# Mamba block on one core: the gate moved behind the transpose of y, with features on partitions

## The chip, the core and the metric

The kernel runs on one core of a Trainium2 chip. The core has a matrix engine (PE, with its weight loads shown apart as PEld), a vector engine (DVE), a scalar engine (ACT), a general engine (POOL) and a queue that issues most transfers (SP). Each engine works through its own instructions in the order in which the program gives them, and waits on semaphores for what the others produce. [...]POOL doesn't read PSUM in this kernel. The metric is the device time of one execution in microseconds (us); lower is better.

## The reference, cut to what matters

The input is x, 8 sequences of 512 tokens with 128 features. After a layer norm, x goes through two branches that are added to it: a bidirectional Mamba block and a mixture of 8 experts. Only the end of the Mamba direction is touched by the change:

```
xz = x @ in_w.T ; xi, z = split(xz)            # 256 features each
xi = silu(causal_conv(xi))
delta, B, C = functions of xi
h[t] = h[t-1] * exp(delta[t] * A) + delta[t] * xi[t] * B[t]    # 16 states per feature
y = sum over states of h * C  +  xi * D
y = y * silu(z)                                 # the gate
out_dir = y @ out_w.T
...
out = concat(out_f, out_b) @ combine_w.T + combine_b + residual
```

The backward direction does the same on the reversed sequence, and its output is reversed again. The experts pick one of eight for each token and compute `down(silu(gate x) * up x)`.

## The kernel before, in words

**Units and steps.** There are 16 units, one for each pair of sequence and direction (unit 0 is the forward direction of sequence 0, unit 1 its backward direction, and so on: even units are forward). A unit has 16 steps, one for each state. In step s the kernel computes for both halves (128 features on partitions, 512 tokens along the free axis) the decays exp(delta*A) on ACT (`decay`, L771), two scans over time on DVE (`scan`, L818), the multiplication by C on POOL (`times_c`, L841, tile hs), and the sum over states on PE: every 128x128 block of hs is transposed and accumulated in PSUM into py (`sum_up`, L855), so that py has tokens on partitions. The scan's other input, the tile b, comes from PE. In odd steps ACT scales blocks (`scaled`, L787, tile dbt) and PE transposes them (L800); in even steps PE spreads a row (L805) and DVE multiplies (`product`, L812). (The first and the last unit split this differently.) ACT, PE's part for b, and the loads of C run up to three steps ahead of the scan.

**The order of the work.** No scheduler moves anything: the loop from L1113 on writes out the order. Beside the state loop a plan holds small jobs for each step and place: "ev" and "ev2" at a step's start, "late" after `scaled(s+3)`, "pe0", "dv" after the step's scans and products, "pe" and "pe2" at its end. Jobs at the same place run in the order in which they were planned: first those of `prepare` (the next unit's inputs), then those of `conclude` (the end of the unit before), then those of the experts.

**Preparing the next unit.** While unit u runs its states, `prepare` builds unit u+1: input transposed (L563, L565, tile xin) and projected (`inner`, L575), the convolution in step 2 at "dv" (`conv`, L590: six DVE instructions), also in step 2 at "pe" the projection of z (`gates`, L599, tile pz), and in step 3 at "ev2" the silus on ACT (`silu`: L608 for u, L610 for z, with table loads around them). Later come px (L619), pd (L650), the logarithm's parts on POOL (L689, L691), delta (L698) and du (L709), and PE's transposes of du (L714).

**Concluding the unit before.** After unit u is summed, in the steps of unit u+1:

- step 2 "dv": `gate`, L881: two DVE multiplications of py (PSUM, tokens on partitions) by z into yt (SBUF). That is the last reader of py, which has a single buffer of two banks.
- steps 3 and 4 "pe2": `back`, four blocks each transposed by PE into pyb: L887 for the forward direction (transposes), L889 for the backward one (a matmul with the exchange matrix, which also reverses the tokens within a block).
- steps 4 and 5 "ev": `back_end`, L906: ACT copies pyb to y.
- steps 7 and 8 "pe": `project`, L914 into po; in forward units each half ends with a one-row float32 matmul that adds the bias (L921).
- step 9 "dv": `total`, L929, adds po to xt.

The last unit has no unit after it and runs the same in two pairs of blocks (`by_pairs`, L931).

**Shared buffers.** All small PE products (pz, pg of the experts, pyb, px, pbt, pd, po, pdu ...) take turns in a pool `ps_mm` of two PSUM banks, in program order. In steps 2 to 5 the order is pz, pz, pg, pyb, px, pyb, pbt. So each of them waits for the reader of the tile two places before it.

**The experts.** From unit 4 on, a group of four tiles of sorted tokens is worked on for each unit. What matters here: in step 3 ("ev", before the z silu) ACT does a table load and a silu over the group (`expert_silu`, L477), PE makes pg (L457) at "pe0" of step 3, and DVE multiplies it in at "dv" of step 4 (`expert_up_end`, L481).

Of the kernel before, what the change touches and what calls it, by code (L numbers as in the profile page):

```python
# [32 lines left out]
F32 = mybir.dt.float32  # L33
BF16 = mybir.dt.bfloat16
I32 = mybir.dt.int32
AF = mybir.ActivationFunctionType
# [19 lines left out]
def columns():  # L56

    at, n = {}, 0
    fields = [("ln_g", 1), ("ln_b", 1), ("rout", E)]
    for d in DIRS:  # L60
        fields += [
            ((d, k), w) for k, w in (
                ("in", 2 * DI), ("conv_w", NH * KC), ("conv_b", NH), ("A_log", NH * NS),
                ("D", NH), ("x", NH * NX),
            )
        ]
    for d in DIRS:
# [9 lines left out]
def block_kernel(ctx: ExitStack, tc: tile.TileContext, a: dict, out: bass.AP):  # L77
    nc = tc.nc
# [17 lines left out]
    def mm(shape, name):  # L96
        return ps_mm.tile(shape, F32, tag="mm", name=name)
# [6 lines left out]
    at, width = columns()  # L104
    pk = const.tile([P, width], F32, name="pk")
# [13 lines left out]
    comb_b = pk[0:1, at["comb_b"]]  # L119
    w = {}  # L120
    for i, d in enumerate(DIRS):
        w[d, "in"] = pk[:, at[d, "in"]]
# [29 lines left out]
    ones = const.tile([P, P], F32, name="ones")  # L152
# [35 lines left out]
    def selector():  # L188


        nothing = const.tile([P, 1], F32, name="nothing")
        nc.vector.memset(nothing, 0.0)
        for k in range(3):
            nc.gpsimd.affine_select(
                out=sel,
                in_=sel if k else nothing[:ROWS].unsqueeze(2).to_broadcast([ROWS, NS, P]), compare_op=ALU.not_equal, fill=1.0,
                base=-k * NS, pattern=[[-1, NS], [0, P]], channel_multiplier=1,
            )

    def project_weights(d, di):  # L200
        mo = const.tile([P, NH, D], F32, name=f"{d}_mo")
        p = mm([P, NH, D], f"pm_{d}")
        for h in range(NH):
            nc.tensor.matmul(
                p[:, h, :], w[d, "out"][:, h * P : (h + 1) * P], comb[:, di, :],
                start=True, stop=True,
            )
        w[d, "mo"] = mo
        return lambda: nc.scalar.copy(mo, p)
# [318 lines left out]
    def prepare(v):  # L528
        b, d = units[v]
# [6 lines left out]
        bank = mm if v else term  # L536
        c = C[v]
# [54 lines left out]
                        cw[:, h, KC - 1 - k : KC - k], c["acc"][:, h, k:], ALU.mult, ALU.add,  # L592
                    )

        def gates(k):
            p = c["pz", k] = bank([P, 2, DI], f"pz_{v}{k}")
            for j in range(2):
                t = (k * 2 + j) * P
                nc.tensor.matmul(  # L599
                    p[:, j, :], c["xin"][:, t : t + P], w[d, "in"][:, DI:],  # L600
                    start=True, stop=True,
                )

        def silu():
            c["z"] = two.tile([P, NJ, DI], F32, tag="z", name=f"z_{v}")
            c["u"] = two.tile([P, NH, L], F32, tag="u", name=f"u_{v}")
            for h in range(NH):
                nc.scalar.activation(c["u"][:, h, :], c["acc"][:, h, :], AF.Silu)  # L608
            for k in range(2):
                nc.scalar.activation(c["z"][:, 2 * k : 2 * k + 2, :], c["pz", k], AF.Silu)  # L610

        def after_silu():

# [109 lines left out]
        do = lambda f, *k: lambda: f(*k)  # L723
# [149 lines left out]
    def conclude(v):  # L873
        b, d = units[v]
        c = C[v]

        def gate(ks=range(0, NJ, 2)):
            if "yt" not in c:
                c["yt"] = tmp.tile([P, NJ, DI], F32, tag="yt", name=f"yt_{v}")
            for k in ks:  # L880
                nc.vector.tensor_mul(  # L881
                    c["yt"][:, k : k + 2], c["py"][:, k : k + 2], c["z"][:, k : k + 2]
                )

        def turned(dst, j, h):
            if d == "f":
                nc.tensor.transpose(dst, c["yt"][:, j, h * P : (h + 1) * P], ident)  # L887
            else:
                nc.tensor.matmul(  # L889
                    dst, c["yt"][:, NJ - 1 - j, h * P : (h + 1) * P], exch,  # L890
                    start=True, stop=True,
                )

        def block(y, h, j):
            return y[:, h, j, :] if len(y.shape) == 4 else y[:, h, j * P : (j + 1) * P]

        def back(h):

            p = c["pyb", h] = mm([P, L], f"pyb_{v}{h}")
            for j in range(NJ):  # L900
                turned(p[:, j * P : (j + 1) * P], j, h)

        def back_end(h):
            if h == 0:
                c["y"] = tmp.tile([P, NH, L], F32, tag="y", name=f"y_{v}")
            nc.scalar.copy(c["y"][:, h, :], c["pyb", h])  # L906

        def project(js=range(NJ), whole=True):
            if whole or js[0] == 0:
                c["po"] = mm([P, NJ, D], f"po_{v}_{js[0]}")  # L910
            p = c["po"]
            for j in js:
                for h in range(NH):
                    nc.tensor.matmul(  # L914
                        p[:, j, :], block(c["y"], h, j), w[d, "mo"][:, h, :],
                        start=(h == 0 and (d == "b" or j == js[0])),
                        stop=(d == "b" and h == NH - 1), skip_group_check=(d == "f"),
                    )
            if d == "f":

                nc.tensor.matmul(  # L921
                    p[:, js[0] : js[-1] + 1, :], ones[0:1, :],
                    comb_b.unsqueeze(1).to_broadcast([1, len(js), D]),
                    start=False, stop=True, skip_group_check=True,
                )

        def total(js=range(NJ)):
            xs = xt[:, b * NJ + js[0] : b * NJ + js[-1] + 1, :]
            nc.vector.tensor_add(xs, c["po"][:, js[0] : js[-1] + 1], xs)  # L929

        def by_pairs():  # L931

            y = tmp.tile([P, NJ, NH, P], F32, tag="y", name=f"y_{v}")
            c["y"] = y.rearrange("p j h t -> p h j t")
            pairs = [range(k, k + 2) for k in range(0, NJ, 2)]
            for i, js in enumerate(pairs):
                gate((NJ - 2 - js[0],) if d == "b" else (js[0],))
                p = c["pyb", i] = mm([P, 2, NH, P], f"pyb_{v}{i}")
# [3 lines left out]
                copy = nc.scalar.copy if i == 0 else nc.vector.tensor_copy  # L942
                copy(y[:, js[0] : js[-1] + 1], p)
# [18 lines left out]

# [49 lines left out]
    for g, ks in enumerate(groups):  # L1012
# [35 lines left out]
    for _ in roots_of_both(nc.vector, 0, NJ):  # L1048
        pass
    weights("f")  # L1050
    selector()
    first.norm()
    first.turn()
    first.turn_end()
# [31 lines left out]
    for h in range(NH):  # L1086
        k = slice(h, h + 1)
# [122 lines left out]
```

## Time and profile before

| | |
|---|---|
| time, median of 3 runs | 952.93 us (952.07 to 959.26) |
| the profiled execution, its own time | 953.34 us |
| its span on the core | 951.6 us |
| busy: DVE / PE / POOL / ACT | 907.2 / 850.2 / 841.5 / 803.0 us |
| mean granted clock of PE | 0.953 |

One execution is profiled. Rows of the timeline give the start, the length, the engine, the source line, what is written and read, how many like instructions were merged, and in brackets how long the engine sat idle before and what released it. Instructions on DVE and ACT overlap a little: the next one starts some 0.1 us before the one before is reported as ended. So the time that an instruction takes from its engine is read from the distance of two starts.

### The profile page before, as it was taken

The page shows a single profiled execution, that of the slowest core. Times are in us where ns is not written, and L with a number is a line of the kernel's source. Part 1 is how long each engine was busy: PE and PEld are TensorE (multiplying, and loading weights), DVE is VectorE, ACT ScalarE, POOL GpSimd, SP SyncE. Part 2 cuts the span into 40 slices and gives each one's busy share as a digit, 9 for nine tenths or more (in the row PEclk, how much of TensorE's full clock was granted, in tenths as well). Part 3 has the DMA queues.
Part 4 walks back from the last instruction along what each step waited for, and adds up shares of the span by engine and source line. Part 5 has one row for each costly group of instructions (what it writes and reads, how often), then busy time and mean ns, then how long its engine had stood idle before and what let it go on. Part 6 is the DMA issues. An engine that isn't in the chain of part 4 may idle for free.

```text
span 951.6 us, 16224 instructions
## 1 busy us (share of the span) xinstructions
PE 850.2 (89%) x5510; PEld 657.9 (69%) x5510; DVE 907.2 (95%) x1101; ACT 803.0 (84%) x1490; POOL 841.5 (88%) x524
## 2 busy tenths in 40 slices
PE   5699896978789889899998999989999999989897
PEld 2367574766567668777786877868777786767676
DVE  7999989999899999999999999999999999999996
ACT  5898986969679797998969989698988979799792
POOL 5689798799999979799897998979899898979995
PEclk9588999988979999999899999999999999999999
DMA  5364222222233625245441544425245341622262
GB/s 153 111 132 107 66 76 66 78 74 80 84 95 104 192 70 182 78 123 163 114 154 53 161 138 121 152 82 185 63 130 168 112 153 54 186 74 85 90 177 75
DMA packets 68483, 108.54 MB, mean 114 GB/s; under 512 B 6848, under 2 KB 29248, under 8 KB 68400
## 3 DMA queue, kind: packets, MB, share of 16 engines
q1 hardware_dynamic: 65552, 101.32, 36.0%
q0 software_dynamic: 2272, 4.67, 1.4%
q10 hardware_dynamic: 576, 1.51, 0.5%
q8 instruction: 44, 0.72, 0.3%
q14 instruction: 39, 0.32, 0.1%
HBM read 97.60 MB, written 9.87 MB: 113 GB/s over the span
## 4 chain that ended last, share of the span: by engine, by line
PE 42%; ACT 26%; DVE 18%; issue 7%; POOL 6%; DMA 1%; SPq 0%; POOLq 0%; DVEq 0%; ACTq 0%
PE py L855 14%; DVE hs L818 10%; ACT dA L771 8%; PE b L800 7%; ACT dbt L787 7%; PE pg L457 4%; PE pd L650 4%; POOL hs L841 3%; DVE b L812 3%; DVE acc L590 2%; PE pde L489 2%; PE po L914 2%; PE b L805 2%; ACT acc L582 1%; PE pdu L714 1%
## 5 line engine op out<-in xcount | busy, mean ns | idle before, releaser
L841 POOL TENSOR_TENSOR hs<-hs,cs 128x1024 f32<-128x1024 f32 x253 | 594.3, 2362 | 71.9 <-DVE hs L818 59.9
L818 DVE TENSOR_TENSOR_SCAN hs<-dA,b 128x512 f32<-128x512 f32 x512 | 592.8, 1206 | 0.1
L855 PE MATMUL py<-ident,hs 128*128 128x128 f32 x2048 | 279.3, 282 | 10.8 <-POOL hs L841 10.7
L855 PEld LDWEIGHTS py<-ident,hs 128*128 128x128 f32 x2048 | 234.4, 145 | 47.2 <-POOL hs L841 23.6
L787 ACT ACTIVATE dbt<-dut,bt 128x256 f32<-128x256 f32 x524 | 221.9, 496 | 0.1
L800 PE MATMUL b<-ident,dbt 128*128 128x128 f32 x1048 | 187.5, 289 | 19.6 <-DVE hs L818 10.4
L771 ACT ACTIVATE dA<-delta,b_A 128x512 f32<-128x512 f32 x256 | 168.2, 715 | 14.9 <-DVE hs L818 14.8
L800 PEld LDWEIGHTS b<-ident,dbt 128*128 128x128 f32 x1048 | 128.8, 145 | 74.1 <-ACT dbt L787 52.7
L771 ACT ACTIVATE dA<-delta,f_A 128x512 f32<-128x512 f32 x256 | 168.6, 715 | 8.3 <-DVE hs L818 6.3
L812 DVE TENSOR_TENSOR b<-du,b 128x512 f32<-128x512 f32 x250 | 159.8, 686 | 9.3 <-PE b L805 8.5
L599 PE MATMUL pz<-pk,xin 128*128 128x256 f32 x128 | 42.8, 492 | 29.3 <-DVE acc L590 25.4
L650 PE MATMUL pd<-cdt,pk 9*128 9x512 f32 x124 | 66.3, 635 | 0.0
L590 DVE SCALAR_TENSOR_TENSOR acc<-pi,pk,acc 128x511 f32<-128x511 f32 (+2 forms) x96 | 64.5, 739 | 0.1
L457 PE MATMUL pg<-xeT,we 128*128 128x128 f32 x468 | 61.8, 278 | 2.2 <-ACT z L610 2.1
L457 PEld LDWEIGHTS pg<-xeT,we 128*128 128x128 f32 x468 | 56.2, 192 | 5.5 <-ACT z L610 3.8
L599 PEld LDWEIGHTS pz<-pk,xin 128*128 128x128 f32 x128 | 30.2, 247 | 41.1 <-ACT dbt L787 26.5
L805 PE MATMUL b<-cdt,sel 48*128 48x512 bf16 x125 | 50.6, 405 | 8.6 <-DVE hs L818 8.6
L721 ACT COPY dut<-pdu 128x512 f32<-128x512 f32 x32 | 18.6, 585 | 34.6 <-PE pdu L714 34.6
L500 POOL DMA_INDIRECT by_token<-ye,to x39 | 39.6, 1016 | 6.3 <-issue 3.1
L646 POOL TENSOR_TENSOR cdt<-cdt 32x512 f32<-32x512 f32 (+1 forms) x32 | 33.1, 1034 | 7.8 <-ACT cdt L632 7.7
L489 PEld LDWEIGHTS pde<-we,g 128*128 128x128 f32 x234 | 27.6, 191 | 15.2 <-issue 7.6
L409 POOL DMA_INDIRECT sorted_in<-xn,row_i x32 | 32.5, 1015 | 5.3 <-issue 3.8
(170 smaller groups left out, 1054.8 us busy)
## 6 DMA issues: line engine op xcount, KB each, us to landing
cs<-cd SPq DMA_DIRECT2D x253, 256.0 KB, 3.5
we<-in_expert_w SPq DMA_DIRECT2D x39, 576.0 KB, 4.6
sorted_in<-empty SPq DMA_DIRECT2D x9, 258.0 KB, 7.9
xe<-sorted_in SPq DMA_DIRECT2D x9, 258.0 KB, 4.5
xt<-in_x SPq DMA_DIRECT2D x8, 256.0 KB, 7.3
moe<-by_token SPq DMA_DIRECT2D x8, 256.0 KB, 3.0
out<-xt SPq DMA_DIRECT2D x7, 256.0 KB, 3.7
pk<-in_pack ACTq DMA_DIRECT2D x1, 704.0 KB, 7.9
```

What stands on the lines that cost most here:

```text
L457: nc.tensor.matmul(p[:, q - 4 * b, :], T[ks[i]][:, which, c, :], G[ks[0], "xT"][:, i, :], start=True, stop=True,)
L590: nc.vector.scalar_tensor_tensor(c["acc"][:, h, k:], c["pi", h][:, : L - k], cw[:, h, KC - 1 - k : KC - k], c["acc"][:, h, k:], ALU.mult, ...
L599: nc.tensor.matmul(p[:, j, :], c["xin"][:, t : t + P], w[d, "in"][:, DI:], start=True, stop=True,)
L650: nc.tensor.matmul(p, w[d, "dt"][:, h * P : (h + 1) * P], cdt[ROW_DT : NX + 1], start=True, stop=True,)
L771: nc.scalar.activation(k["dA"][:, h, :], c["delta"][:, h, :], AF.Exp, scale=w[d, "A"][:, h, n : n + 1],)
L787: nc.scalar.activation(k["dbt"][:, j, :], c["dut"][:, j, :], AF.Copy, scale=c["bt"][:, j, n : n + 1],)
L800: nc.tensor.transpose(k["b", h][:, j * P : (j + 1) * P], k["dbt"][:, j, h * P : (h + 1) * P], ident,)
L805: nc.tensor.matmul(k["b", 0], sel[:, n, :], c["bc"], start=True, stop=True)
L812: nc.vector.tensor_mul(k["b", h], c["du"][:, h, :], k["b", 0])
L818: nc.vector.tensor_tensor_scan(k["hs"][:, h, :], k["dA"][:, h, :], k["b", h], 0.0, ALU.mult, ALU.add)
L841: nc.gpsimd.tensor_mul(k["hs"], k["hs"], k["cs"].unsqueeze(1).to_broadcast([P, NH, L]))
L855: nc.tensor.matmul(c["py"][:, j, h * P : (h + 1) * P], block[:, h, j * P : (j + 1) * P], weight, skip_group_check=True, **kw,)
```

## The change

The gate is applied after the transpose instead of before it.

- `gates(h)` computes z with features on partitions: the weights are stationary and xin is moving, two matmuls 512 wide in place of four 256 wide. z then has the layout of u (features by tokens), and three buffers instead of two.
- `leave` (step 2, "late") copies py to yt by one ACT instruction over both banks. DVE no longer has a job for the unit before in step 2.
- `back` uses transposes in both directions; the exchange matrix is no longer used here.
- `gate(h)` (steps 4 and 5, "dv") is a DVE multiplication of pyb (PSUM) by z into y. For the backward direction y is written from its last token to its first. It replaces ACT's copies L906.
- `project` starts in forward units with a single matmul of three rows in bf16 over all four blocks, in place of the two float32 matmuls at the end of the halves. The three rows are the bias split in three bf16 pieces, made once at the start by two small POOL subtractions (`bias_pieces`); the packed input holds the bias in three rows.
- `by_pairs` follows the same order for the last unit: two copies out of py (one on ACT, one on DVE), the transposes, two DVE multiplications.

```diff
+    bias = comb_b.bitcast(BF16).rearrange("p (n two) -> p n two", two=2)[:, :, 1]
+    one_row = const.tile([3, P], BF16, name="one_row")
+    nc.gpsimd.memset(one_row, 1.0)
...
+    def bias_pieces():
+        for m in (2, 1):
+            nc.gpsimd.tensor_sub(comb_b[:m], comb_b[:m], bias[:m])
...
-        def gates(k):
-            p = c["pz", k] = bank([P, 2, DI], f"pz_{v}{k}")
-            for j in range(2):
-                t = (k * 2 + j) * P
-                nc.tensor.matmul(
-                    p[:, j, :], c["xin"][:, t : t + P], w[d, "in"][:, DI:],
-                    start=True, stop=True,
-                )
+        def gates(h):
+            p = c["pz", h] = bank([P, L], f"pz_{v}{h}")
+            nc.tensor.matmul(
+                p, w[d, "in"][:, DI + h * P : DI + (h + 1) * P], c["xin"],
+                start=True, stop=True,
+            )
...
-            c["z"] = two.tile([P, NJ, DI], F32, tag="z", name=f"z_{v}")
+            c["z"] = two.tile([P, NH, L], F32, tag="z", name=f"z_{v}", bufs=3)
...
-        def gate(ks=range(0, NJ, 2)):
+        def leave(copy=nc.scalar.copy, js=range(NJ)):
             if "yt" not in c:
                 c["yt"] = tmp.tile([P, NJ, DI], F32, tag="yt", name=f"yt_{v}")
-            for k in ks:
-                nc.vector.tensor_mul(
-                    c["yt"][:, k : k + 2], c["py"][:, k : k + 2], c["z"][:, k : k + 2]
-                )
+            k = slice(js[0], js[-1] + 1)
+            copy(c["yt"][:, k], c["py"][:, k])
 
         def turned(dst, j, h):
-            if d == "f":
-                nc.tensor.transpose(dst, c["yt"][:, j, h * P : (h + 1) * P], ident)
-            else:
-                nc.tensor.matmul(
-                    dst, c["yt"][:, NJ - 1 - j, h * P : (h + 1) * P], exch,
-                    start=True, stop=True,
-                )
+            nc.tensor.transpose(dst, c["yt"][:, j, h * P : (h + 1) * P], ident)
...
-        def back_end(h):
+        def gate(h):
             if h == 0:
                 c["y"] = tmp.tile([P, NH, L], F32, tag="y", name=f"y_{v}")
-            nc.scalar.copy(c["y"][:, h, :], c["pyb", h])
+
+            y = c["y"][:, h, :] if d == "f" else c["y"][:, h, ::-1]
+            nc.vector.tensor_mul(y, c["pyb", h], c["z"][:, h, :])
...
+            if new and d == "f":
+
+                nc.tensor.matmul(
+                    p, one_row, bias.unsqueeze(1).to_broadcast([3, NJ, D]),
+                    start=True, stop=False, skip_group_check=True,
+                )
...
-            (2, "dv", gate),
-            (3, "pe2", do(back, 0)), (4, "ev", do(back_end, 0)),
-            (4, "pe2", do(back, 1)), (5, "ev", do(back_end, 1)),
+            (2, "late", leave),
+            (3, "pe2", do(back, 0)), (4, "dv", do(gate, 0)),
+            (4, "pe2", do(back, 1)), (5, "dv", do(gate, 1)),
```

More of the change, by code (lines that the diff above doesn't have):

```diff
@@ L118, in block_kernel @@
     comb = halves("comb", D)
-    comb_b = pk[0:1, at["comb_b"]]
+    comb_b = pk[0:3, at["comb_b"]]
+    bias = comb_b.bitcast(BF16).rearrange("p (n two) -> p n two", two=2)[:, :, 1]
+    one_row = const.tile([3, P], BF16, name="one_row")
+    nc.gpsimd.memset(one_row, 1.0)
     w = {}
@@ L608, in silu @@
                 nc.scalar.activation(c["u"][:, h, :], c["acc"][:, h, :], AF.Silu)
-            for k in range(2):
-                nc.scalar.activation(c["z"][:, 2 * k : 2 * k + 2, :], c["pz", k], AF.Silu)
+            for h in range(NH):
+                nc.scalar.activation(c["z"][:, h, :], c["pz", h], AF.Silu)
         def after_silu():
@@ L875, in conclude @@
         c = C[v]
-        def gate(ks=range(0, NJ, 2)):
+        def leave(copy=nc.scalar.copy, js=range(NJ)):
             if "yt" not in c:
                 c["yt"] = tmp.tile([P, NJ, DI], F32, tag="yt", name=f"yt_{v}")
-            for k in ks:
-                nc.vector.tensor_mul(
-                    c["yt"][:, k : k + 2], c["py"][:, k : k + 2], c["z"][:, k : k + 2]
-                )
+            k = slice(js[0], js[-1] + 1)
+            copy(c["yt"][:, k], c["py"][:, k])
         def turned(dst, j, h):
-            if d == "f":
-                nc.tensor.transpose(dst, c["yt"][:, j, h * P : (h + 1) * P], ident)
-            else:
-                nc.tensor.matmul(
-                    dst, c["yt"][:, NJ - 1 - j, h * P : (h + 1) * P], exch,
-                    start=True, stop=True,
-                )
-        def block(y, h, j):
-            return y[:, h, j, :] if len(y.shape) == 4 else y[:, h, j * P : (j + 1) * P]
+            nc.tensor.transpose(dst, c["yt"][:, j, h * P : (h + 1) * P], ident)
         def back(h):
@@ L901, in back @@
                 turned(p[:, j * P : (j + 1) * P], j, h)
-        def back_end(h):
+        def gate(h):
             if h == 0:
                 c["y"] = tmp.tile([P, NH, L], F32, tag="y", name=f"y_{v}")
-            nc.scalar.copy(c["y"][:, h, :], c["pyb", h])
+            y = c["y"][:, h, :] if d == "f" else c["y"][:, h, ::-1]
+            nc.vector.tensor_mul(y, c["pyb", h], c["z"][:, h, :])
         def project(js=range(NJ), whole=True):
-            if whole or js[0] == 0:
+            new = whole or js[0] == 0
+            if new:
                 c["po"] = mm([P, NJ, D], f"po_{v}_{js[0]}")
             p = c["po"]
+            if new and d == "f":
[3 more added lines that the diff above has]
+                )
             for j in js:
@@ L914, in project @@
                     nc.tensor.matmul(
-                        p[:, j, :], block(c["y"], h, j), w[d, "mo"][:, h, :],
-                        start=(h == 0 and (d == "b" or j == js[0])),
-                        stop=(d == "b" and h == NH - 1), skip_group_check=(d == "f"),
-                    )
[L919 to L925, printed above, removed]
+                        p[:, j, :], c["y"][:, h, j * P : (j + 1) * P], w[d, "mo"][:, h, :],
+                        start=(d == "b" and h == 0), stop=(h == NH - 1),
+                        skip_group_check=(d == "f"),
+                    )
         def total(js=range(NJ)):
@@ L931, in by_pairs @@
         def by_pairs():
-            y = tmp.tile([P, NJ, NH, P], F32, tag="y", name=f"y_{v}")
-            c["y"] = y.rearrange("p j h t -> p h j t")
+            c["y"] = tmp.tile([P, NH, L], F32, tag="y", name=f"y_{v}")
+            blocks = lambda t: t.rearrange("p h (j t) -> p j h t", t=P)
             pairs = [range(k, k + 2) for k in range(0, NJ, 2)]
-            for i, js in enumerate(pairs):
-                gate((NJ - 2 - js[0],) if d == "b" else (js[0],))
-                p = c["pyb", i] = mm([P, 2, NH, P], f"pyb_{v}{i}")
+            late = pairs[::-1]
+            for i, js in enumerate(late):
+                leave(nc.vector.tensor_copy if i else nc.scalar.copy, js)
+            for i, js in enumerate(late):
+                k = slice(js[0], js[-1] + 1)
+                p = mm([P, 2, NH, P], f"pyb_{v}{i}")
                 for j in js:
@@ L941, in by_pairs @@
                         turned(p[:, j - js[0], h, :], j, h)
-                copy = nc.scalar.copy if i == 0 else nc.vector.tensor_copy
-                copy(y[:, js[0] : js[-1] + 1], p)
+                nc.vector.tensor_mul(
+                    blocks(c["y"][:, :, ::-1])[:, k], p, blocks(c["z"])[:, k]
+                )
             for js in pairs:
@@ L1051, in block_kernel @@
     selector()
+    bias_pieces()
     first.norm()
@@ L1180 @@
         pack[NX, c] = v["dt_b"]
-    pack[0, at["comb_b"]] = inputs[pre + "combine_b"]
+    pack[:3, at["comb_b"]] = inputs[pre + "combine_b"]
     src["pack"] = pack
```

## The prediction

> **What bounds the kernel now.** I read the page's busy shares first, then DVE's waits, then one unit boundary in the timeline, then POOL's starts against the scans.
>
> ```profile
> PE 850.2 (89%) x5510; PEld 657.9 (69%) x5510; DVE 907.2 (95%) x1101; ACT 803.0 (84%) x1490; POOL 841.5 (88%) x524
> ...
> DVE b L812 <- PE b L805: 8.5, 15, 0.9
> DVE yt L881 <- PE py L855: 2.7, 3, 1.6
> ```
>
> DVE idles 44.4 us of 951.6. By windows of about a unit, 8.6 of that lie in the first 48 us and 8.7 in the last 22; a unit in the middle has 1 to 4. An edit that only moves DVE work can therefore win little, but anything that makes DVE wait costs. The gate hardly waits now (2.7 us in three places).
>
> The boundary at 681 us, in the middle of the run (unit 10, forward, is concluded in unit 11), engine by engine:
>
> ```profile
> 681.18 1.28 DVE L881 TENSOR_TENSOR yt<-py,z 128x512 f32<-128x512 f32 x2
> 682.38 1.21 DVE L818 TENSOR_TENSOR_SCAN hs<-dA,b 128x512 f32<-128x512 f32 x1
> ...
> 688.03 0.67 DVE L481 TENSOR_TENSOR g<-g,pg 128x512 f32<-128x512 f32 x1
> 688.61 1.22 DVE L818 TENSOR_TENSOR_SCAN hs<-dA,b 128x512 f32<-128x512 f32 x1
> ...
> 681.37 1.28 ACT L477 ACT_TABLE_LOAD   x1
> 682.66 1.49 ACT L477 ACTIVATE g<-g 128x1536 f32<-128x1536 f32 x1
> 684.05 1.14 ACT L608 ACTIVATE u<-acc 128x512 f32<-128x512 f32 x2
> 685.09 1.06 ACT L610 ACTIVATE z<-pz 128x512 f32<-128x512 f32 x2
> ...
> 685.72 1.16 PE L457 MATMUL pg<-xeT,we 128*128 128x128 f32 x8
> 686.72 0.60 PE L800 MATMUL b<-ident,dbt 128*128 128x128 f32 x4
> 687.15 0.60 PE L887 MATMUL pyb<-ident,yt 128*128 128x128 f32 x4
> 688.01 1.09 PE L855 MATMUL py<-ident,hs 128*128 128x128 f32 x8
> 688.94 1.45 PE L619 MATMUL px<-u,pk 128*104 128x512 f32 x3
> ```
>
> The reader is to see a chain: ACT goes through table load, expert silu, u and z without a pause; pg starts 0.05 us after the first z (685.67), as it needs that pz bank; b and pyb follow back to back, ready at 687.75. Today only ACT waits for pyb.
>
> **The change, part by part.**
>
> *DVE.* The two multiplications leave step 2 (distance of starts 682.38 - 681.18 = 1.20 us) and two of the same shape come at steps 4 and 5: 0.68 us each as in L881, since an operand in PSUM, one in SBUF and the size stay. Writing backwards is in no row: 0.68 is the nearest row; twice that is my upper end (0.68 x 16 = 11 us), below 0.68 is excluded since the elements are the same. I take 0.68.
>
> *ACT.* Two copies L906 (distance to the next start 0.47 each) go, one of 1024 from PSUM comes. Its row doesn't exist: a 512 copy takes 578 ns, and the SBUF activations L666 went from 630 (512) to 1058 (1024), so 578 + 428 = 1.01 us, less 0.12 overlap = 0.89 on the engine; 0.8 to 1.0 as ends. The total is nil, but the place isn't: it stands in step 2 ahead of the table load. Queued behind it are the expert silu, u and z, and behind z wait PE's pg, b and pyb. It doesn't wait itself: py's last sum ended at 678.1, ACT comes free at 681.37.
>
> *The new wait.* With the copy, z's first half ends at 685.67 + 0.89 = 686.56, pg starts at 686.61, pyb 1.43 later as now (687.15 - 685.72), takes 0.60, and DVE can multiply at 688.69. DVE arrives at 688.03 - 1.20 = 686.83. Stall: 1.85 us; behind it are L481, which also frees the bank for px, and all scans. For a backward unit (boundary at 625) the same: pg 629.53, pyb 630.96, DVE 631.83 - 1.20, as pyb there falls to 0.60 too. At the second multiplication DVE comes 3.4 us of scans and products later, pyb is there.
>
> *What the stall is worth.* Two counts. DVE idles 0.92 us (at 666.96) in the unit from 625 to 681 and 0.37 + 0.24 + 0.46 = 1.07 in the next; these waits are for PE and vanish when DVE is late: 1.85 - 0.92 = 0.93 and 1.85 - 1.07 = 0.78 remain. POOL: from step 5 to the end of du it is busy without a break, and its waits elsewhere show that hs starts 0.24 after the scan at the earliest. In step 7 it starts 1.13 after (698.89 against 697.77), so 0.89 is free and 0.96 of the 1.85 goes on, to du, to PE, which already waits for it in the unit from 625, to xin, to ACT, and to the next boundary:
>
> ```profile
> 664.99 0.66 PE L714 MATMUL pdu<-ident,du 128*128 128x128 f32 x4 [0.50 <-POOL du L709]
> ```
>
> I take 0.95 for a boundary that concludes a backward unit and 0.80 for a forward one, where POOL's du leaves PE 0.15 more.
>
> *PE.* Backward pyb: transposes instead of exchange matmuls. Rows: eight records in 1.06 us against four in 0.60. The Trainium skill (TensorE: Matmul & The Clock Gate, Part 4: PE-mode transpose) puts a transpose in a kernel at about 275 ns and says that it doesn't count as busy for the clock gate: four would be 1.1 us, no gain, with 0.5 more stall in backward units (5 x 0.5 = 2.5 us) and a lower clock. The rows decide: four end to end in 0.60, and the stretch from 629 to 679, mostly transposes, ran at a granted clock of 1.00. Bias: 0.69 twice becomes one three-row bf16 matmul 512 wide, nearest row L805 at 405 ns (0.25 to 0.63 as ends): 0.9 us less in each forward unit. But px now waits for L481: 688.69 + 1.26 = 689.95 against 688.94, 1.0 later. So PE is even at du and the gain is spent. pz: 8 records 1.97, as L575 with 4 records 1.88: nil. If POOL didn't hold PE there, the 0.9 would come out; that is the second rival.
>
> The Trainium skill (Perfetto Trace Analysis, Matmuls) asks to rotate PSUM banks so that evacuation overlaps the next matmuls. pyb is now evacuated by the late DVE and px stands behind; the rule has no price, the row gives the 1.0 above.
>
> *Start.* A memset and two POOL subtractions (nearest POOL rows 0.1 and 0.24 to 0.40) stand behind the selector, where POOL idles 7.7 us until 22.08: nil; uncovered 0.9 us.
>
> **Sum.** Boundaries with an expert silu: units 4 to 13, ten. The first has DVE 0.5 later against ACT, so stall 1.26; there POOL's slack is nil (hs starts 0.23 after the scan) and I take 1.0. Then five backward at 0.95 (4.75) and four forward at 0.80 (3.2): 8.95 in all. The boundaries of units 0 to 3: the first delays POOL by about 1 (logits stand where pg does); the second lets POOL start its saturated stretch 1.2 earlier (171 us) as the gate no longer precedes the scan; the third stalls DVE about 1.1, but DVE idles 4.0 us for POOL at 257. I take 0. Unit 14: 0. Tail: now 943.46 gate, 947.30 first total, 948.23 second. New: copies on ACT and DVE side by side to 944.1, transposes 0.6, multiplication 0.68 to 945.5, four blocks of project 1.06, total at 946.6, the second at 947.65: -0.6.
>
> Span 951.6 + 8.95 - 0.6 = 960.0. The profiled execution took 953.34, 1.7 around the span, so 961.7; the median lies 0.4 below the profiled one: 961 us, 0.9% slower.
>
> **Rivals.**
> - *The stall is paid whole.* DVE is 95% busy and recovers nothing: 10 x 1.85 + 1.3 + 1.1 - 0.6 = +20, 973 us. For: DVE has no idle in many units' first 30 us. Against: the idles that vanish are counted above and are waits for PE. A dearer backward write or copy ends here too.
> - *Faster: PE and POOL set the pace.* POOL starts step 3's product 1.2 earlier, PE saves 0.9 in a forward unit and 0.9 (two times 0.46) in a backward one. If the stall stays below POOL's free 0.89, nothing of it passes on and about 0.9 in 14 units less 0.6 comes out: 940 us. The price falls on POOL's step 7; the point is a stall of 0.9. It would need z to leave ACT 1 us sooner than counted. For: PE is busy without a gap from 685.7 to 735.6. Against: ACT's chain from xin to z has no pause in the row.
> - *Nothing moves.* Slack unseen takes the rest (DVE's 27 us of idle outside start and tail): 953.
>
> **How the numbers follow.** Forecast 0.52, whole stall 0.20, nothing 0.18, faster 0.10. A measurement of this kernel can tell about 1% (9.5 us) from no change; the forecast at 961 lies just inside that, and some 0.2 of its 0.52 beyond. So slower 0.41, same 0.50, faster 0.09. The range: forecast with its ends (0.4 to 1.4 for a boundary: 956 to 967), stretched to the nothing case below and most of the whole stall above: 952 to 972.
>
> **What would show it.** DVE's gate on pyb idle some 1.3 to 1.9 us before it, for PE, at ten boundaries, none at units 1 and 3. ACT's copy of 1024 near 1.0 us without a wait. POOL no longer 3 to 3.7 us idle at step 3 but less, and 1 us at steps 5 or 7. Fewer waits DVE b L812 for PE. px 1 us later against pg. The second total 0.6 earlier against the last scan. Wrong if gate has no wait (then the faster rival), if DVE's idle rises by 20 us (the first), or if writing backwards costs more than 0.7 us.

## The result, and the profile after

The changed kernel takes 968.54 us (median of 4 runs, 966.91 to 968.99) against 952.5 us for the kernel before (median of 4): a ratio of 1.0157, 95% interval 1.0132 to 1.0182. The forecast was 961.0 (952 to 972). The sign and the range hold; the loss is 16 us where 8 were forecast. The profiled execution of the changed kernel took 968.78 us, its span is 967.0 us, 15.4 us more than before.

The page of the changed kernel: the busy line, and the groups of POOL's product and of DVE's new gate (count, busy us, mean ns, then idle just before them and what ended it).

```profile
PE 848.2 (88%) x5358; PEld 643.7 (67%) x5358; DVE 907.3 (94%) x1101; ACT 806.5 (83%) x1475; POOL 843.0 (87%) x527
...
L848 POOL TENSOR_TENSOR hs<-hs,cs 128x1024 f32<-128x1024 f32 x253 | 594.3, 2360 | 88.0 <-DVE hs L825 72.3
...
L904 DVE TENSOR_TENSOR y<-pyb,z 128x512 f32<-128x512 f32 x30 | 20.4, 679 | 25.8 <-PE pyb L891 25.8
```

No engine has noticeably more to do. DVE's busy time is 907.3 against 907.2, so its idle time went from 44.4 to 59.7 us, and the 15.3 between them is the difference of the spans to 0.1. The gate alone waits 25.8 us where it waited 2.7, so 23.1 us of new waiting came in and 7.8 us of other waiting went. What went are waits for PE and POOL, above all those of L698 (L705 now) for POOL: 6.1 us before, 2.5 now. DVE's longest waits now (us in all, times, longest):

```profile
DVE y L904 <- PE pyb L891: 25.8, 14, 3.4
DVE b L819 <- PE b L812: 7.4, 10, 1.7
DVE st L236 <- DMA xt<-in_x: 5.2, 2, 5.0
```

The boundary that stood at 681 us is at 692.6 now (unit 10 concluded in unit 11). The timeline of the changed kernel, ACT, DVE and PE after one another:

```profile
692.62 0.99 ACT L888 COPY yt<-py 128x1024 f32<-128x1024 f32 x1
693.62 1.28 ACT L486 ACT_TABLE_LOAD   x1
694.92 1.49 ACT L486 ACTIVATE g<-g 128x1536 f32<-128x1536 f32 x1
696.31 1.14 ACT L615 ACTIVATE u<-acc 128x512 f32<-128x512 f32 x2
697.35 1.06 ACT L617 ACTIVATE z<-pz 128x512 f32<-128x512 f32 x2
...
694.84 3.44 DVE L825 TENSOR_TENSOR_SCAN hs<-dA,b 128x512 f32<-128x512 f32 x3
700.05 0.69 DVE L904 TENSOR_TENSOR y<-pyb,z 128x512 f32<-128x512 f32 x1 [1.77 <-PE pyb L891]
700.66 0.68 DVE L490 TENSOR_TENSOR g<-g,pg 128x512 f32<-128x512 f32 x1
...
697.98 1.16 PE L466 MATMUL pg<-xeT,we 128*128 128x128 f32 x8 [0.92 <-ACT z L617]
698.97 0.60 PE L807 MATMUL b<-ident,dbt 128*128 128x128 f32 x4
699.41 0.60 PE L891 MATMUL pyb<-ident,yt 128*128 128x128 f32 x4
...
701.20 1.88 PE L626 MATMUL px<-u,pk 128*104 128x512 f32 x4
```

The copy stands ahead of everything, z comes 0.89 us later than before (counted from the end of the convolution: 5.30 against 4.41), PE has run out of other work and waits 0.92 us for z, pg and pyb follow, and DVE, which has given up the two multiplications and is early, stands 1.77 us at the gate. This is the chain of the forecast, with its durations.

Where the 15.4 us lie can be read from the ends of the convolutions in the two timelines, one per unit. Up to the one at 343.10 (before: 341.26) it is +1.84, in the nine periods from there to 866.13 (850.76) +13.53, and from there to the end +0.03. The nine periods follow (f or b: direction of the unit concluded). Beside them stand the stretches in which PE's granted clock was 0.5 instead of 1.0 (3.41 us long, or a multiple), counted where they start 4.7 to 20 us after the convolution, while pyb, px and pd are made. Those at the boundary itself, within 1 us of the convolution's end, are not counted:

| period | before, us | such stretches | after, us | such stretches |
|---|---|---|---|---|
| unit 4, f | 56.13 | | 58.43 | 1 |
| 5, b | 56.20 | | 58.76 | 2 |
| 6, f | 58.29 | 1 | 57.65 | |
| 7, b | 56.47 | 1 | 57.17 | |
| 8, f | 56.72 | | 60.05 | 2 |
| 9, b | 56.19 | | 57.46 | 1 |
| 10, f | 56.72 | | 58.46 | 1 |
| 11, b | 56.17 | | 57.43 | 1 |
| 12, f | 56.61 | | 57.62 | |

Without such a stretch a forward period went from 56.72 to 57.65 (+0.93; unit 12 has +1.01) and a backward one from 56.19 to 57.17 (+0.98). That gives 5 x 0.93 + 4 x 0.98 = 8.6 of the 13.5, about 5 us less than was measured. The changed kernel has a stretch in six of nine periods, the kernel before in two. Held against the periods of the same kernel and direction without one, the six are 6.1 us longer and the two 1.8, so 4.3 of the 5 us lie in the stretches. (The rest is unit 4, which was 0.6 us shorter than the other forward periods before.) One such stretch, at unit 10, and the 3.4 us ahead of it at full clock, as windows of the trace (us, busy us of PE, PEld, DVE, ACT, POOL with instructions, granted clock, DMA share, GB/s):

```profile
706.70:710.10 3.40, 3.40 (x16) 1.84 (x16) 3.40 (x5) 3.11 (x8) 3.40 (x3) 1.00 0.86 253
710.20:713.40 3.20, 3.20 (x16) 2.85 (x15) 3.20 (x4) 3.14 (x5) 2.63 (x2) 0.50 0.71 182
```

The page's mean clock fell from 0.953 to 0.938.

### The profile page after: what moved, and what is told of

The parts are those of the page before. It is cut to its first block, busy times and chain, and to the rows that moved or that the text cites. A ratio compares the mean times of both kernels' runs of the same rounds, so it can differ in the third digit from the quotient of the medians.

```text
span 967.0 us, 15927 instructions
## 1 busy us (share of the span) xinstructions
PE 848.2 (88%) x5358; PEld 643.7 (67%) x5358; DVE 907.3 (94%) x1101; ACT 806.5 (83%) x1475; POOL 843.0 (87%) x527
## 4 chain that ended last, share of the span: by engine, by line
PE 43%; ACT 27%; DVE 18%; issue 7%; POOL 3%; DMA 2%; SPq 0%; DVEq 0%; POOLq 0%; ACTq 0%
PE py L862 14%; DVE hs L825 10%; ACT dA L778 8%; ACT dbt L794 7%; PE b L807 7%; PE pd L657 4%; PE pg L466 4%; PE pde L498 3%; DVE b L819 2%; PE b L812 2%; PE po L919 2%; POOL hs L848 2%; ACT acc L591 2%; ACT g L486 2%; ACT u L615 1%
## 5 line engine op out<-in xcount | busy, mean ns | idle before, releaser
L862 PE MATMUL py<-ident,hs 128*128 128x128 f32 x2048 | 285.7, 286 | 15.3 <-POOL hs L848 14.3
L862 PEld LDWEIGHTS py<-ident,hs 128*128 128x128 f32 x2048 | 240.3, 148 | 63.7 <-issue 32.6
L778 ACT ACTIVATE dA<-delta,b_A 128x512 f32<-128x512 f32 x256 | 167.8, 714 | 17.7 <-DVE hs L825 17.5
L807 PEld LDWEIGHTS b<-ident,dbt 128*128 128x128 f32 x1048 | 132.1, 149 | 68.3 <-ACT dbt L794 32.3
L466 PE MATMUL pg<-xeT,we 128*128 128x128 f32 x468 | 64.0, 285 | 16.6 <-ACT z L617 16.6
L466 PEld LDWEIGHTS pg<-xeT,we 128*128 128x128 f32 x468 | 58.3, 198 | 19.0 <-ACT z L617 18.9
L606 PE MATMUL pz<-xin,pk 128*128 128x512 f32 x64 | 42.0, 792 | 29.0 <-DVE acc L599 22.9
L812 PE MATMUL b<-cdt,sel 48*128 48x512 bf16 x125 | 50.5, 404 | 17.9 <-DVE hs L825 17.6
L904 DVE TENSOR_TENSOR y<-pyb,z 128x512 f32<-128x512 f32 x30 | 20.4, 679 | 25.8 <-PE pyb L891 25.8
L606 PEld LDWEIGHTS pz<-xin,pk 128*128 128x128 f32 x64 | 13.3, 227 | 45.4 <-ACT dbt L794 29.3
```

What stands on the lines that cost most here:

```text
L466: nc.tensor.matmul(p[:, q - 4 * b, :], T[ks[i]][:, which, c, :], G[ks[0], "xT"][:, i, :], start=True, stop=True,)
L778: nc.scalar.activation(k["dA"][:, h, :], c["delta"][:, h, :], AF.Exp, scale=w[d, "A"][:, h, n : n + 1],)
L807: nc.tensor.transpose(k["b", h][:, j * P : (j + 1) * P], k["dbt"][:, j, h * P : (h + 1) * P], ident,)
L812: nc.tensor.matmul(k["b", 0], sel[:, n, :], c["bc"], start=True, stop=True)
L862: nc.tensor.matmul(c["py"][:, j, h * P : (h + 1) * P], block[:, h, j * P : (j + 1) * P], weight, skip_group_check=True, **kw,)
```

## The experiments

Three theories were to be told apart. The first (A): DVE's stall at the gate is the cost, so it goes when DVE has something else to do there. The rival (D): ACT's copy, queued ahead of the expert silu, u and z, makes z and all that PE does behind it late, and that costs even if DVE doesn't stall. And the clock (B): PE's gaps at the boundary lead to more half-clock stretches, and these make up the part above the forecast. Besides, the parts of the change that were costed at nothing (PE's transposes, the bias) should be seen by themselves. To compare with the table above, the nine periods of each run's profile are given as a sum (before 509.5 us, after 523.0).

### The gates one step later

```diff
-            (3, "pe2", do(back, 0)), (4, "dv", do(gate, 0)),
-            (4, "pe2", do(back, 1)), (5, "dv", do(gate, 1)),
+            (3, "pe2", do(back, 0)), (5, "dv", do(gate, 0)),
+            (5, "pe2", do(back, 1)), (6, "dv", do(gate, 1)),
```

> The changed kernel with DVE's two gates one step later (5 and 6) and the second half of the transposes at step 5. Theory A (the wait of the gate for pyb is the loss): the gate's idle falls from 25.8 us to under 5, and the time falls from 968 to 950 to 956. Theory B (half of the loss is PE, whose granted clock halves more often): the gate's idle falls as well, but the half-clock stretches remain, and the time stays near 960.

Measured: 964.44 us (961.28 to 966.01), ratio 1.0113 (1.0086 to 1.014). Nine periods 518.7. The list of DVE's waits:

```profile
DVE g L490 <- PE pg L466: 12.8, 10, 1.9
DVE b L819 <- PE b L812: 10.7, 16, 1.7
DVE y L904 <- PE pyb L891: 5.6, 14, 1.7
```

Theory A had 950 to 956 and missed; theory B had near 960, and 10 half-clock stretches after 340 us remain. The gate's wait is nearly gone, but the expert multiplication, which is now the first in the queue, waits for pg at ten boundaries: pg is as late as z. Of the 13.5 us in the nine periods 9.2 stay. In the two periods without any half-clock stretch past the boundary itself (574.35 to 631.64 and 689.03 to 746.36, both forward) it is +0.57 and +0.61 against +0.93. So the stall at this one line isn't the cause, only one place where lateness shows.

### The copy out of py made twice

```diff
             k = slice(js[0], js[-1] + 1)
+            if v < len(units) - 1:
+                copy(c["yt"][:, k], c["py"][:, k])
             copy(c["yt"][:, k], c["py"][:, k])
```

> The changed kernel with ACT's copy of py made twice, so that z comes another 0.89 us later. Theory A: the gate waits 0.9 us longer at each of some 14 boundaries, idle 25.8 to about 37 us, time 968 to 976 to 981. Theory B: a longer wait matters only as far as PE's clock goes with it; under 3 us.

Measured: 984.31 us (982.48 to 987.43), ratio 1.0342 (1.0314 to 1.0371), some 16 us more than the changed kernel and above the 976 to 981 of theory A; theory B's under 3 us is out. z comes 6.35 after the convolution (+1.05), the gate waits 39.7 us in all (+13.9), the nine periods sum to 539.1 (+16.1), which is 1.8 us for each 1.05 of ACT. The clock falls to 0.93, with 19 half-clock stretches after 340 us against 13, so this sum holds stretches as well. A second copy costs as much as the first or more: no slack is left.

### The same time on ACT in the kernel before, twice

First as a copy of py that nobody uses:

```diff
+        def leave():
+            t = tmp.tile([P, NJ, DI], F32, tag="extra", name=f"extra_{v}")
+            nc.scalar.copy(t, c["py"])
+
...
-            (2, "dv", gate),
+            (2, "late", leave), (2, "dv", gate),
```

> The kernel before with an additional ACT copy of py at the same place (its result is not used), so ACT is as late with z as in the changed kernel, but DVE doesn't wait for pyb. Theory A: below 3 us more than before, as the chain through z has about 0.9 us to spare before DVE needs pg (pg would end at 687.8 against DVE's 688.03 at the boundary of unit 10). Rival (ACT's or PE's delay alone is the loss, whoever gates): 8 us or more.

Measured: 975.07 us (974.22 to 975.87), ratio 1.0232 (1.0214 to 1.0249). It doesn't answer the question, as DVE's waits show:

```profile
DVE yt L881 <- ACT extra L887: 15.9, 13, 3.6
```

DVE's gate reads the same tile as the copy and was made to wait for it, though both only read. The edit added a wait in place of ACT time alone. So it was done again with a copy of the same size from SBUF, which touches nothing that DVE needs:

```diff
+        def aside():
+            t = tmp.tile([P, NH, L], F32, tag="aside", name=f"aside_{v}")
+            nc.scalar.copy(t, c["delta"])
+
...
-            (2, "dv", gate),
+            (2, "late", aside), (2, "dv", gate),
```

> The kernel before with an extra ACT copy of 1024 elements per partition at the place of the new copy, out of an SBUF tile into an unused one, so that only ACT (and z) comes about 0.95 us later; DVE's gate is untouched. The gate on the copy's bank, which made the run with an extra copy out of py wait 1.0 us on DVE thirteen times, is gone. Theory A (only DVE's wait for pyb costs): under 3 us more than before. Rival D (the chain through ACT to z and pg is itself the loop that sets the period): 6 to 12 us more, with DVE waiting for pg or for PE's spreading.

Measured: 963.93 us (959.53 to 965.97), ratio 1.0127 (1.0087 to 1.0167); nine periods 518.5. DVE's waits:

```profile
DVE w L678 <- PE one L685: 9.4, 6, 2.0
DVE b L812 <- PE b L805: 7.5, 11, 1.5
...
DVE yt L881 <- PE py L855: 2.5, 2, 1.7
DVE g L481 <- PE pg L457: 2.0, 5, 0.4
```

Here the gate is in its old place and doesn't wait, and DVE's scan of step 7 ends where it always did (16.6 us after the convolution, before: 16.51). Still the time rose by 1.3%. The lateness goes through PE, which waits for z at the boundary (here at 456 us, where unit 6 is concluded; before, at unit 10, it didn't wait there):

```profile
461.68 1.16 PE L457 MATMUL pg<-xeT,we 128*128 128x128 f32 x8 [0.60 <-ACT z L610]
```

After the convolution z comes at 5.34 (+0.93), the column "one" at 18.47 (17.53), the first pdu at 38.14 (37.20), xin at 48.77 (47.83). PE works without a gap over 0.1 us from pg on, and passes the 0.93 on whole. Forward periods without a half-clock stretch past the boundary grew by 0.93 (57.66 and 57.65 against 56.72), backward ones by 0.08 (56.27, 56.27 and 56.26 against 56.19), as PE had time there. That gives 5 x 0.93 + 4 x 0.08 = 5.0 of the 9.0 us by which the nine periods grew; the other 4.0 are mostly half-clock stretches (in units 4, 8 and 9 here, in 6 and 7 before). So theory D holds in forward units, though not by the sign that it named: DVE's waits for pg and for the spreading are much as before (2.0 and 7.5 us against 1.5 and 8.5), and new is the one for "one". In backward units the late z alone costs 0.08, where the changed kernel loses 0.98: there the loss needs DVE's stall. The lateness of z has two ways to the next boundary, over DVE and over PE. Closing one leaves the other.

### The z silu ahead of the experts' silu

This takes the lateness away in the changed kernel and keeps all else: the table load now comes before u, and the expert silu after z.

```diff
-            (3, "ev2", silu), (3, "ev2", after_silu),
+            (3, "ev", silu), (3, "ev2", after_silu),
```

> The changed kernel with u's and z's silus ahead of the experts' silu in step 3, so that z leaves ACT 1.4 us earlier; all else as changed. Theory A and D alike: the gate's wait falls from 1.77 to about 0.9 us (PE then holds pg), below POOL's 0.89 of slack, so most of the loss goes: 955 to 960. If the loss came from anything behind the gates (clock, PE order), 965 or more.

Measured: 951.22 us (949.52 to 960.48, 12 runs), ratio 0.9995 (0.9972 to 1.0018). The same boundary in its timeline:

```profile
680.90 1.00 ACT L888 COPY yt<-py 128x1024 f32<-128x1024 f32 x1
681.92 1.28 ACT L615 ACT_TABLE_LOAD   x1
683.21 1.15 ACT L615 ACTIVATE u<-acc 128x512 f32<-128x512 f32 x2
684.27 1.07 ACT L617 ACTIVATE z<-pz 128x512 f32<-128x512 f32 x2
685.23 1.49 ACT L486 ACTIVATE g<-g 128x1536 f32<-128x1536 f32 x1
...
687.15 0.69 DVE L904 TENSOR_TENSOR y<-pyb,z 128x512 f32<-128x512 f32 x1 [0.58 <-PE pyb L891]
...
685.18 1.06 PE L466 MATMUL pg<-xeT,we 128*128 128x128 f32 x8
```

z is there 3.93 after the convolution, pg starts here without a wait, and the gate stalls 0.58 us instead of 1.77 (0.39 at other boundaries, 8.8 us in all). The nine periods sum to 506.1, 3.4 under the kernel before, and the time is below the 955 to 960 that was expected. The lateness of z thus holds the whole loss. The half-clock stretches of the table go with it: one of the nine periods has one, where the changed kernel has them in six. (The page's mean clock doesn't tell: it is 0.941, near the changed kernel's 0.938; over the nine periods it is 0.98 against 0.96.) The stall of 0.58 is under POOL's free 0.89 that the forecast read, and indeed nothing of it passes: the scan of step 7 ends 0.5 to 0.7 later than before, but POOL's product of step 7 starts 17.24 to 17.44 after the convolution where it started at 17.63.

Does this edit help by itself? The same line in the kernel before:

> The kernel before with u's and z's silus ahead of the experts' silu, the edit that brought the changed kernel back to the time of before. If that edit worked there by ending the wait for z (theory A and D), it is worth little here, where nothing waits for z any longer than for other things: 949 to 954. If it is a gain by itself, 935 to 943, and then the changed kernel still loses its 16 us.

Measured: 955.6 us (950.76 to 962.14, 20 runs), ratio 1.0027 (1.0009 to 1.0046). z is earlier there too (3.03 after the convolution), but pg isn't (3.8 to 4.4 after it), because PE comes to pg only then. So the edit gains nothing in the kernel before (it is 0.3% slower, if anything, and just above the 949 to 954 expected), and undoes in the changed kernel what the copy did.

With the first gate also moved behind the expert multiplication, which is ready earlier:

```diff
-            (3, "ev2", silu), (3, "ev2", after_silu),
+            (3, "ev", silu), (3, "ev2", after_silu),
...
-            (3, "pe2", do(back, 0)), (4, "dv", do(gate, 0)),
+            (3, "pe2", do(back, 0)), (5, "ev", do(gate, 0)),
```

> The same, and in addition the first gate stands behind the experts' multiplication on DVE instead of ahead of it. Theory A and D: DVE has 0.6 us of work while pyb comes, the waits fall to 0.3 to 0.5 us, 949 to 956; under it, the savings on PE may show. If the bank that px waits for is what costs, the gain is larger than the wait's fall of 0.5 us at 10 boundaries, below 950.

Measured: 950.33 us (947.09 to 953.87, 12 runs), ratio 0.9983 (0.9967 to 0.9999); DVE's waits:

```profile
DVE y L904 <- PE pyb L891: 4.0, 3, 2.9
```

The gate waits only three times. It is the fastest of all that ran, by 0.2% against the kernel before, with an interval that just leaves out no change.

### PE's part alone

The kernel before, with transposes in both directions in all units but the last (ACT's copy then writes backwards) and the bias in three bf16 rows instead of the two float32 matmuls; the gate stays in step 2.

```diff
-            if d == "f":
+            if d == "f" or v < len(units) - 1:
...
-            nc.scalar.copy(c["y"][:, h, :], c["pyb", h])
+            y = c["y"][:, h, :] if d == "f" else c["y"][:, h, ::-1]
+            nc.scalar.copy(y, c["pyb", h])
...
+            if new and d == "f":
+                nc.tensor.matmul(
+                    p, one_row, bias.unsqueeze(1).to_broadcast([3, NJ, D]),
+                    start=True, stop=False, skip_group_check=True,
+                )
```

> The kernel before with only the parts that save PE time: transposes in both directions (ACT's copy of pyb writes the backward y in reverse) and the bias as one three-row bf16 matmul. The gate stays in step 2 on DVE. If PE sets the pace between pg and the next boundary, as its unbroken row suggests, 0.9 us in each unit: 940 to 948. If POOL or DVE hold PE anyway: 950 to 954.

Measured: 952.64 us (949.01 to 957.6, 19 runs), ratio 1.0 (0.9984 to 1.0016). PE's busy time is 838.7 us (850.2 before); the 11.5 us less are worth nothing that can be seen. The clock of the profiled execution is 0.957 (before 0.953).

### PE kept busy at the boundary

In the changed kernel, repeated matmuls whose result is the same, so that PE waits less for the convolution and for z. The spread of a row is made five times, the transposes for step 5 twice in one kernel and four times in another; the edit of the latter:

```diff
-            for j in range(NJ):
+            for j in list(range(NJ)) * (4 if (n, h) == (5, 0) and s > 2 * NS else 1):
...
-            nc.tensor.matmul(k["b", 0], sel[:, n, :], c["bc"], start=True, stop=True)
+            for _ in range(5 if n == 4 and s > 2 * NS else 1):
+                nc.tensor.matmul(k["b", 0], sel[:, n, :], c["bc"], start=True, stop=True)
```

> The changed kernel with repeated PE work in the idle times of the boundaries: the spreading matmul for step 4 five times instead of once (1.6 us in the wait for the convolution), the first four transposes for step 5 twice (0.6 us in the wait for z). Theory B: fewer half-clock stretches after 340 us than the 13 of the changed kernel, and 3 to 6 us less: 962 to 965. Theory A: the clock has no part, 967 to 971.

Measured with two: 968.37 us (967.21 to 970.67), ratio 1.0168 (1.0145 to 1.019), clock 0.945. There are 9 half-clock stretches after 340 us instead of 13, but the time isn't shorter, and the nine periods sum to 523.2.

> As the run named warm, with the first four transposes for step 5 made four times (1.3 us of PE work in the wait for z, after 1.6 us in the wait for the convolution). [...]Theory B: no such stretch is left at most boundaries, at most 4 half-clock stretches after 340 us, and the periods of the units fall to what those without a half-clock stretch had (0.9 and 0.7 us above before): 961 to 964. If the clock has no part in the loss: 967 to 971.

Measured with four: 967.85 us (967.47 to 971.42), ratio 1.0162 (1.012 to 1.0203), clock 0.949. Eight stretches after 340 us are left where at most 4 were expected. The nine periods as windows of the trace (columns as above), first of the changed kernel:

```profile
343.00:866.00 523.00, 482.41 (x3205) 378.07 (x3204) 499.25 (x568) 451.51 (x808) 460.62 (x256) 0.96 0.39 122
```

and of the one with fourfold transposes:

```profile
345.00:865.00 520.00, 492.20 (x3349) 385.41 (x3348) 499.47 (x567) 451.18 (x808) 460.55 (x256) 0.98 0.39 123
```

The clock came back to 0.98, which is what the kernel before has in its nine periods, and the sum fell by 2.7 us, to 520.3. The loss of 10.8 against the kernel before stays. The last three periods, which hold no stretch, take 57.64, 57.16 and 57.64 us, as those without one in the changed kernel do (57.65, 57.17 and 57.62): the 0.93 and 0.98 are lost at full clock as well. The other six hold one, 16.8 to 17.5 us after the convolution, and are 0.3 us (backward) or 0.8 us (forward; 0.9 at unit 4) longer. Over all runs the gain isn't seen: the ratio is 1.0162, the changed kernel's 1.0157.

## Why the prediction was right, and where its size was off

**The new wait.** Forecast 1.85 us at ten boundaries; measured 1.76 or 1.77 at six of the ten boundaries of units 4 to 13 and 1.45 at unit 13. At units 0 to 3 it waited 2.81, 0.70, 0.27 and 0 (expected: none at units 1 and 3). The three others of the ten (2.57 at unit 4, where 1.26 was forecast, 3.12 and 3.37 at units 5 and 8) had a half-clock stretch on pg and pyb. The pieces were right: copy 0.99 (forecast 1.01), z +0.89 (0.89), gate 2.07 after the start of pg (2.08), multiplication 679 ns forwards and backwards together (684 before), so that a dearer reversed write is excluded.

**What the stall is worth.** Forecast 0.95 for a backward unit and 0.80 for a forward one, or 1.0 + 4 x 0.95 + 4 x 0.80 = 8.0 for the nine periods. Measured +0.98 and +0.93 where no half-clock stretch intervenes, 8.6 in all. So this term was sized right (the two directions came out nearly equal), and in periods without a half-clock stretch its route was the one forecast, over DVE and POOL: POOL's free 0.89 in step 7 was used up, the product of step 7 starts 18.61 after the convolution instead of 17.63, 0.23 after its scan, and PE then waits for POOL's du. The transposes of du in a forward unit, in the kernel before (unit 10) and in the changed one (unit 6):

```profile
721.30 0.60 PE L714 MATMUL pdu<-ident,du 128*128 128x128 f32 x4
...
501.21 0.66 PE L721 MATMUL pdu<-ident,du 128*128 128x128 f32 x4 [0.21 <-POOL du L716]
```

That is 40.9 us after the convolution instead of 40.0. PE's own row, which carries the 0.93 in the run with ACT's time alone, stands just behind as a second way.

**The step that was off: "PE is even at du and the gain is spent".** It took PE's durations at the clock of the boundary shown and put a change of that clock at nothing. Without a stretch PE isn't even: its first pdu comes 0.50 later in forward units (37.70 after the convolution, before 37.20) and 1.34 later in backward ones (37.70, before 36.36), but it then waits for POOL, so this costs nothing. With a stretch PE sets the time: at unit 10 the first pdu comes at 38.93 and doesn't wait for POOL. Half-clock stretches after 340 us went from 7 to 13, those that count in the table from two of nine periods to six, and 4.3 of the 13.5 us lie in them.

What brings them stays open. In the changed kernel PE stands 1.89 us for the convolution and then, in units 5 to 12, 0.9 or 2.6 for z. Before, at the boundaries of units 9 and 10, what came after the first wait was 1.5 us in two waits in the backward unit and 0.1 in the forward one. But the eight stretches of the six periods don't follow these gaps alone. Three start right after 3.41 us in which PE idled 2.0 to 2.5 us; units 5, 7 and 8 have the same two gaps, and only units 5 and 8 have the stretch. The other five start 13.7 or 17.1 us after an earlier stretch, and PE had idled at most 0.40 us in the 3.41 us before them. Removing the lateness of z removed all but one of them; filling the gaps left six periods with one.

**The sum.** The forecast had 8.35 us more of span, measured are 15.4. The nine periods make +0.6 in the stall and +4.9 above it, the part before 341 us +1.84, the rest -0.3. That 968.5 lies in the range is luck in part: the room above 967 was left for a stall that is paid whole, and not for what came.

The Trainium skill (TensorE: Matmul & The Clock Gate, Part 4: PE-mode transpose) says that transposes don't count as busy for the clock gate, which would have been another reason for a lower clock. PE's part alone has the transposes, but for the last unit, and a clock of 0.957, so they aren't it; and four of them took 0.60 us again, not the 1.1 that would be estimated from the page's price.

**The early boundaries, taken at 0,** show +1.84 us. But this part of the run scatters: the other variants of the changed kernel reach the convolution of unit 6 at 339.27 (copy twice) to 344.99 us (fourfold transposes), before at 341.26. So no cost can be read there.

**PE's savings** (0.9 us per unit) came to nothing, as forecast: PE's part alone has the ratio 1.0. The bias matmul took 450 ns, inside the bounds of 0.25 to 0.63:

```profile
L888 ACT COPY yt<-py 128x1024 f32<-128x1024 f32 x15 | 15.0, 998 | 1.0 <-PE py L862 1.0
...
L913 PE MATMUL po<-pk,one_row 3*128 3x512 bf16 x8 | 3.6, 450 | 0.0
```

(groups of the changed kernel by shape: count, busy us, mean ns, idle before.)

**Of the signs that were named,** px 1 us later against pg was a slip: in the forecast's own sum pg moves as well. Against pg it stands 3.22 us later in both kernels, against the convolution 8.58 instead of 7.68, so +0.90 where 1.0 was summed. Waits for L812 (L805 before) became fewer, 10 instead of 15, with 7.4 us instead of 8.5. POOL's idle at step 3 fell to 1.8 in forward units and 2.5 in backward ones, and it waits 1.62 and 0.57 in steps 5 and 7. The tail's 0.6 us can't be seen: from the last convolution to the end it is 100.9 us in both, and DVE waits 2.3 us there for ACT's half of the copy.

**The rivals.** The stall paid whole (973) didn't come: of 23.1 us new waiting at the gate 7.8 were recovered elsewhere. "PE and POOL set the pace" named its point, a stall under 0.9, and its condition, z a microsecond sooner. The z silu moved ahead brought both about; the step worked, but with 0.3 to 0.5 us per period instead of 0.9, so 951 and not 940.

## What to carry to other kernels

A job that gets a new place in an engine's queue isn't free, even if the engine's total stays the same: ask what is queued behind the new place. Here 0.9 us of copy in each unit, on an engine that is busy 84% of the time, cost 1.6%, since it stood ahead of the activation that PE's next work waits for; letting that activation pass an earlier job in the queue gave all of it back. Before a wait that the profile shows is taken away, look what the next instruction of that queue waits for: where it is the same late producer, the wait only changes its line.

## What the runs showed of the hardware that was not expected

- The granted clock of PE in these traces has two values, 1.0 and 0.5, and changes in windows of 3.41 us. How many fall in an execution varies for one kernel: the mean clock of the kernel before ran from 0.943 to 0.958. One on pg and pyb made the gate's stall 3.1 to 3.4 us instead of 1.77, and those that began 16 to 19 us after a convolution, before and after, did so though PE had idled at most 0.40 us in the 3.41 us ahead of them.
- A second, unused reader of a PSUM tile on ACT made the reader on DVE wait for it, 15.9 us at 13 boundaries. Whether the chip needs that or only the program's own semaphores ask for it was not tried.
